# A graph layer in two convolutions: the first table holds max(x − mean, 0), and 1/std moves to a scale column

## The chip, the cores and the metric

One core of one Trainium2 chip. The metric is device time in microseconds (us) for one execution of the whole program. A core has five engines that run their own instruction streams beside each other: PE (TensorE, matmuls), DVE (VectorE), ACT (ScalarE), POOL (GpSimd, here the issuer of gathers) and SP (SyncE, here the issuer of all other DMAs).

## The reference

The input is x (6250 nodes × 512), and 100000 edges as src and dst, sorted by dst. With h = relu(layernorm(x)), deg the number of edges that leave a node, dinv = 1/sqrt(deg) and 0 where deg is 0, the program computes

```python
norm = -dinv[src] * dinv[dst]
prop = lambda h: segment_sum(h[src] * norm[:, None], dst)
a = h @ W1_0 + prop(h) @ W1_1 + b1
a = layer_norm(a) * gamma + beta
a = where(a >= 0, a, 0.01 * a)
out = x + a @ W2_0 + prop(a) @ W2_1 + b2
```

All of it is float32.

## The kernel before, in words

**Tiles.** The nodes are 49 blocks of 128 (the last has 106 rows), the edges 782 chunks of 128. Each of the two convolutions ("layers") has a table in DRAM with one row per node. Table 0 has rows of 512 + 16 floats: the row of h, and behind it a scale column, one float of which is used. Both layers run over the edges in order: POOL gathers the table rows of a chunk's 128 sources with one indirect DMA (L482), DVE makes a selection matrix for three chunks at a time that already holds the source's scale (L613 and on), PE sums the gathered rows into nodes by matmul (L668) and places the sums in blocks of nodes (L701); then each block is multiplied by the two weight matrices (L571), gets its bias and its layer norm (L754 to L785), and is stored into table 1.

**The prologue**, up to some 155 us, has to make the degrees, the layer norm of x, and table 0. x is loaded into places in SBUF in nine groups of blocks: 2, 4, 4, 4, 7, 7, 7, 7 and 6 (load_x, L185).

- *Degrees.* A loop of 25 iterations (L361 to L383, index g) counts src in two digits. Each makes two one-hot tiles on DVE (lo and hi, L365), and 16 matmuls on PE (both_ps, L382). Two buffers of one-hot tiles are in use, so DVE of iteration g + 2 waits for PE of iteration g. At g = 1 PE and ACT turn the src ids into per-partition indices for the gathers (turn_rest, L294: transposes L242, copies sidx L244), at g = 2 the dst ids (turn_dst, L298).
- *Statistics.* For the first 31 blocks ACT makes them (stats, L264): one pass for the sum (L269), one for the sum of squares (L273), then a square root for the group (L275). DVE turns this into 1/std and −mean/std (spread, L277: L280 and L281). For the last 18 blocks DVE makes them after the loop with bn_stats (L407 to L418).
- *Table.* make_table (L283) does relu(x · rs + nb) in place on ACT with a scale and a bias per node (L289), then SP stores two blocks at a time (L290), and then POOL may gather raw rows of x into the places just stored (gather_raw, L251). The first 76 chunks are gathered from x itself in this way, before the table is there; after the scales are known, the look-ups (L521 to L542) find the scale and bias of each of these rows and ACT applies relu to them.
- *Turns.* At certain iterations of the degree loop one group is finished: spread, make_table, one more load (load_rest), statistics of the group two further on. The dictionary at L339 gives them: iteration 1 the group 0, 4 the group 1, 7, 11, 17 and 21 the groups 2 to 5. The rest of the 31 blocks follows behind the loop.
- *Scales.* Behind the loop the counts are folded into deg; root = sqrt(max(deg, 1)) on ACT (L400), dinv, ndinv = −dinv and other columns on DVE. Then come the 18 other blocks, one DMA that writes dinv into the scale column of the first 31 blocks (L420, 3968 elements of 4 bytes), and the two products sc = (rs · dinv, nb · dinv) for the look-ups (L421 and L422). The column of the other 18 blocks is put into their places ahead of the store (L417).

**What sets the order.** On SP every DMA goes in the order in which the program issues it, and a waiting one holds those behind it. SP's order at the start is: x group 0, src ids, group 1, src ids by chunk, group 2, dst ids by chunk, groups 3, 4 and 5; after that what the turns issue. load_rest(k) loads group 6 + k for k below 3. It is called as load_rest(k − 1) in the turns k = 0 to 3, that is with −1, 0, 1 and 2. On ACT and DVE a scheduler interleaves the operations around the loop by priority; behind the prologue the orders of PE, POOL and SP are written out by hand.

**In layer 0** the scaled sum of a block is copied on ACT with the factor ndinv per node (an, L799), multiplied by W1_1 on top of h times W1_0, and DVE adds the bias (L768; for the last four blocks, which are begun early, L592).

Of the kernel before, what the change touches and what calls it, by code (L numbers as in the profile page):

```python
# [21 lines left out]
P = 128  # L22
# [22 lines left out]
def gnn_kernel(  # L45
# [71 lines left out]
    ndeg = const.tile([P, NB], F32, name="ndeg")  # L117
    ln = const.tile([P, 2, NB], F32, name="ln")
    dlx = const.tile([P, 1 + STEP * NQ * NS + 1], F32, name="dlx")
# [85 lines left out]
    load_end(chunks[1], dst)  # L205
    for i0, n in groups[3:6]:
        load_x(i0, n)

    def load_rest(k):
        if k < 3:  # L210
            load_x(*groups[6 + k])
        if k == 2:
            nc.sync.dma_start(tab[1][zero_row : zero_row + 1, :], places[P - 1 : P, RE + NB - 1, :D])
        for t, w in zip(w_sb[k - 3 : k - 2], (W1_1, W1_0)[k - 3 :]) if k >= 3 else ():
            nc.sync.dma_start(t, w.rearrange("(k p) d -> p k d", p=P))
        if k == 4:
            for t, v in ((bias1, b1), (bias2, b2), (gam, gamma), (bet, beta)):
                nc.sync.dma_start(t, dup(v, P))
# [39 lines left out]

    rs_all, nb_all = ln[:, 0, :], ln[:, 1, :]
    nm_all = ep.tile([P, NB], F32, name="nm_all")  # L260
    sq_all = ep.tile([P, NB], F32, name="sq_all")
    sums = ep.tile([P, NB], F32, name="sums")

    def stats(i0, n):  # L264

        cols = slice(i0, i0 + n)
        for i in range(i0, i0 + n):
            junk = ep.tile([P, D], BF, name="junk")
            nc.scalar.activation(junk, places[:, RE + i, :D], AF.Copy, accum_out=sums[:, i : i + 1])  # L269
        nc.scalar.activation(nm_all[:, cols], sums[:, cols], AF.Copy, scale=-1.0 / D)  # L270
        for i in range(i0, i0 + n):
            junk = ep.tile([P, D], BF, name="junk")
            nc.scalar.activation(junk, places[:, RE + i, :D], AF.Square, bias=nm_all[:, i : i + 1],  # L273
                                 accum_out=sq_all[:, i : i + 1])
        nc.scalar.activation(rs_all[:, cols], sq_all[:, cols], AF.Sqrt, bias=eps, scale=1.0 / D)  # L275

    def spread(i0, n):  # L277

        cols = slice(i0, i0 + n)
        nc.vector.reciprocal(rs_all[:, cols], rs_all[:, cols])  # L280
        nc.vector.tensor_mul(nb_all[:, cols], nm_all[:, cols], rs_all[:, cols])  # L281

    def make_table(i0, n):  # L283

        for lo in range(i0, i0 + n, 2):
            hi = min(lo + 2, i0 + n)
            for i in range(lo, hi):
                v = places[:, RE + i, :D]
                nc.scalar.activation(v, v, AF.Relu, bias=nb_all[:, i : i + 1], scale=rs_all[:, i : i + 1])  # L289
            nc.sync.dma_start(tab[0][lo * P : hi * P, :].rearrange("(i p) d -> p i d", p=P),  # L290
                              places[:, RE + lo : RE + hi, :])
            gather_raw(X + RE + lo, X + RE + hi)
# [45 lines left out]
    assert len(groups) == 9 and all(n > 0 for _, n in some + others)  # L338
    turns = {1: 0, 4: 1, 7: 2, 11: 3, 17: 4, 21: 5}  # L339
    with tc.issue_after(turned.ins):  # L340
        for k in range(2):
            stats(*some[k])

    both = ep.tile([P, NB, 2, 2], F32, name="both")
    with tc.tile_pool(name="deg", bufs=1) as dp, tc.tile_pool(name="onehot", bufs=2) as ohp, tc.tile_pool(
# [15 lines left out]
        for g in range(EJ // (2 * GJ)):  # L361
# [9 lines left out]
            if k is not None:  # L371
                spread(*some[k])
                make_table(*some[k])
                if k < 4:
                    load_rest(k - 1)
                if k + 2 < len(some):
                    stats(*some[k + 2])
            if g in (1, 2):
                with tc.tile_pool(name="turn_ps", bufs=3 - g, space=bass.MemoryType.PSUM) as wps:
                    (turn_rest, turn_dst)[g - 1](wps)  # L380
            for j in range(GJ):
# [3 lines left out]

    spread(*some[6])
    make_table(*some[6])

# [18 lines left out]
    for i0, n in others:  # L407
        cols = slice(i0, i0 + n)
        st = ep.tile([P, 7, 6], F32, name="st")
        mv = ep.tile([P, 7, 2], F32, name="mv")  # L410
        for j in range(n):
            nc.vector.bn_stats(st[:, j, :], places[:, RE + i0 + j, :D])
# [3 lines left out]
        nc.vector.scalar_tensor_tensor(nb_all[:, cols], mv[:, :n, 0], -1.0, rs_all[:, cols], op0=OP.mult, op1=OP.mult)  # L416
# [4 lines left out]
    nc.vector.tensor_mul(sc[:, 0, :], rs_all, dinv)  # L421
    nc.vector.tensor_mul(sc[:, 1, :], nb_all, dinv)  # L422

# [9 lines left out]
def usual_path(tc, have):  # L433
    nc = tc.nc
    (x, out, tab, root, ndeg, ndinv, sidx, dlx, iota_r, w_sb, W2_1, W2_0, w_late, ident, eps, ones, first, nodes_ps, node_of, minus,
     unsorted, dinv, sdinv, bias1, bias2, gam, bet, unseen, unit, N, E, D, NB, NC, NU, NS, KD, rows, places, R,
     load_rest, sc, pick, src_lo, src_hi, eidx, e_src, zero_row, p_id, lent, X, starts, src, W) = (
        have[n] for n in ("x out tab root ndeg ndinv sidx dlx iota_r w_sb W2_1 W2_0 w_late ident eps ones first nodes_ps node_of "
                          "minus unsorted dinv sdinv bias1 bias2 gam bet unseen unit N E D NB NC NU NS KD rows places "
# [13 lines left out]
    with ExitStack() as es:  # L453
# [131 lines left out]
        def early(layer, i):  # L585
# [5 lines left out]
            if layer == 0:  # L591
                nc.vector.tensor_add(pre[i][:r], u_ps[:r], bias1[:r])  # L592
# [161 lines left out]
        def finish(layer, i, v):  # L754
            r = rows[i]
            v = v[:r]
            if layer == 1:
# [8 lines left out]
                return  # L766
            if i < NB - 1:
                nc.vector.tensor_add(v, v, pre.pop(i)[:r] if i in EARLY else bias1[:r])  # L768
            st = pool.tile([P, 6], F32, name="st")
# [17 lines left out]
        def turn(layer, i, left=()):  # L787
# [7 lines left out]
            for k, aT in left:  # L795
# [565 lines left out]
```

## Time and profile before

| what | value |
|---|---|
| median of 3 runs | 2463.06 us (2460.94 to 2464.36) |
| the profiled execution: its own time | 2480.21 us |
| the profiled execution: its span | 2478.4 us |
| mean granted PE clock | 0.836 |

The profile comes from one further execution, with the profiler on. Its span runs from the first instruction to the last; 1.8 us of the execution's own time lie around it. Start times are counted from the start of the span. A row of the timeline gives start, duration, engine, line, operation, the tiles written and read, and in brackets how long the engine had been idle and what released it. A row of the groups gives busy us and mean ns, then the idle time ahead of them and its releasers. "places" are the blocks of x, the table rows and the gathered rows in turn; q1 is the queue of SP's DMAs, q0 that of the gathers.

### The profile page before, as it was taken

The page shows a single profiled execution, that of the slowest core. Times are in us where ns is not written, and L with a number is a line of the kernel's source. Part 1 is how long each engine was busy: PE and PEld are TensorE (multiplying, and loading weights), DVE is VectorE, ACT ScalarE, POOL GpSimd, SP SyncE. Part 2 cuts the span into 40 slices and gives each one's busy share as a digit, 9 for nine tenths or more (in the row PEclk, how much of TensorE's full clock was granted, in tenths as well). Part 3 has the DMA queues.
Part 4 walks back from the last instruction along what each step waited for, and adds up shares of the span by engine and source line. Part 5 has one row for each costly group of instructions (what it writes and reads, how often), then busy time and mean ns, then how long its engine had stood idle before and what let it go on. Part 6 is the DMA issues. An engine that isn't in the chain of part 4 may idle for free.

```text
span 2478.4 us, 19802 instructions
## 1 busy us (share of the span) xinstructions
PE 1719.3 (69%) x6907; PEld 710.0 (29%) x6907; DVE 678.2 (27%) x1449; ACT 390.7 (16%) x703; POOL 1494.4 (60%) x1578
## 2 busy tenths in 40 slices
PE   4567768576776766767766576766777767677788
PEld 3443223222222222223322122222232222222333
DVE  5954323132333322323333111111121111111121
ACT  5864111110111111111110000000010101000001
POOL 5455656666666666656645566666666666666560
PEclk7768878788888887889887688878889888888899
DMA  9885667667766776767645676766767677676670
GB/s 343 305 275 162 203 181 213 201 196 210 214 209 191 212 216 201 212 185 225 193 142 155 180 226 208 226 199 215 220 208 230 211 227 218 202 228 222 204 224 32
DMA packets 183086, 515.60 MB, mean 208 GB/s; under 512 B 33858, under 2 KB 35632, under 8 KB 182976
## 3 DMA queue, kind: packets, MB, share of 16 engines
q0 software_dynamic: 125120, 415.88, 56.5%
q1 hardware_dynamic: 57816, 98.34, 11.4%
q8 instruction: 56, 0.92, 0.1%
q14 instruction: 54, 0.44, 0.1%
q10 hardware_dynamic: 40, 0.02, 0.0%
HBM read 475.25 MB, written 38.86 MB: 207 GB/s over the span
## 4 chain that ended last, share of the span: by engine, by line
PE 33%; another core or an unknown queue 22%; issue 22%; POOL 9%; DVE 8%; DMA 4%; ACT 1%; DVEq 0%; SPq 0%; POOLq 0%; ACTq 0%
PE u_ps L571 16%; POOL places L482 9%; PE ps L668 8%; PE an_ps L701 5%; DMA places<-tab,sidx 2%; DMA places<-tab,lidx 2%; PE hT_ps L807 1%; PE hT_ps L559 1%; DVE aT L809 1%; DVE hi L365 1%; DVE there L689 1%; PE hT_ps L530 1%; DVE sel L613 1%; DVE lo L365 1%
## 5 line engine op out<-in xcount | busy, mean ns | idle before, releaser
L482 POOL DMA_INDIRECT places<-tab,sidx x1191 | 1136.5, 954 | 661.6 <-issue 304.8
L668 PE MATMUL ps<-places,sel 128*32 128x512 f32 x3104 | 426.1, 643 | 20.2 <-issue 19.6
L701 PE MATMUL an_ps<-agg,there 128*128 128x512 f32 (+1 forms) x554 | 277.0, 629 | 128.3 <-issue 91.7
L482 POOL DMA_INDIRECT places<-tab,lidx x270 | 256.0, 948 | 142.7 <-issue 67.9
L571 PE MATMUL u_ps<-w,aT 128*128 128x512 f32 x384 | 205.3, 684 | 154.2 <-DVE aT L809 91.0
L571 PE MATMUL u_ps<-places,aT 128*128 128x512 f32 x384 | 211.2, 700 | 130.0 <-DVE aT L809 110.6
L613 DVE TENSOR_TENSOR sel<-dlx,nodes_ps 128x384 f32<-128x384 f32 (+3 forms) x134 | 72.4, 542 | 699.0 <-remote 586.1
L571 PE MATMUL u_ps<-w,hT 128*128 128x512 f32 (+1 forms) x400 | 203.6, 655 | 34.4 <-ACT hT L561 30.1
L681 ACT ACTIVATE agg<-ps 128x512 f32<-128x512 f32 (+2 forms) x130 | 76.4, 590 | 950.0 <-remote 722.2
L571 PE MATMUL u_ps<-places,hT 128*128 128x512 f32 (+2 forms) x408 | 197.0, 629 | 16.8 <-ACT hT L561 16.2
L668 PEld LDWEIGHTS ps<-places,sel 128*32 128x32 f32 x3104 | 98.8, 116 | 326.8 <-issue 301.2
L701 PEld LDWEIGHTS an_ps<-agg,there 128*128 128x128 f32 (+1 forms) x554 | 104.7, 198 | 253.9 <-issue 221.5
L807 PE MATMUL hT_ps<-ident,an 128*128 128x128 f32 x384 | 69.6, 309 | 126.0 <-issue 65.1
L571 PEld LDWEIGHTS u_ps<-w,aT 128*128 128x128 f32 x384 | 81.0, 221 | 260.3 <-issue 154.8
L689 DVE TENSOR_SCALAR there<-iota_r,node_of 128x128 f32<-128x128 f32 (+1 forms) x286 | 82.3, 295 | 253.5 <-remote 115.6
L571 PEld LDWEIGHTS u_ps<-places,aT 128*128 128x128 f32 x384 | 82.5, 226 | 239.1 <-DVE aT L809 126.5
L561 ACT ACTIVATE hT<-hT_ps 128x512 f32<-128x512 f32 (+1 forms) x98 | 58.3, 595 | 449.7 <-remote 144.8
L571 PEld LDWEIGHTS u_ps<-w,hT 128*128 128x128 f32 (+1 forms) x400 | 80.6, 212 | 121.4 <-issue 90.0
L762 DVE SCALAR_TENSOR_TENSOR u_ps<-u_ps,root,bias 128x512 f32<-128x512 f32 x45 | 34.1, 759 | 289.1 <-issue 124.6
L571 PEld LDWEIGHTS u_ps<-places,hT 128*128 128x128 f32 (+1 forms) x408 | 80.4, 208 | 99.2 <-issue 81.1
L807 PEld LDWEIGHTS hT_ps<-ident,an 128*128 128x128 f32 x384 | 44.7, 152 | 209.8 <-issue 133.0
L253 POOL DMA_INDIRECT places<-in_x_dram,sidx x63 | 60.2, 955 | 68.3 <-issue 18.7
(196 smaller groups left out, 1217.9 us busy)
## 6 DMA issues: line engine op xcount, KB each, us to landing
h<-tab SPq DMA_DIRECT2D x90, 256.0 KB
places<-tab,sidx POOLq DMA_INDIRECT x1191
xt<-in_x_dram SPq DMA_DIRECT2D x48, 256.0 KB
out_dram<-t SPq DMA_DIRECT2D x48, 256.0 KB
tab<-t SPq DMA_DIRECT2D x46, 256.0 KB
tab<-places SPq DMA_DIRECT2D x22, 528.0 KB
places<-in_x_dram SPq DMA_DIRECT2D x5, 1792.0 KB
places<-tab,lidx POOLq DMA_INDIRECT x270
```

The lines of the kernel that those rows point to most:

```text
L253: nc.gpsimd.indirect_dma_start(out=lent[t] if t < X else places[:, t - X, :D], out_offset=None, in_=x, in_offset=bass.IndirectOffsetOnAxis ...
L365: nc.vector.tensor_tensor(t, s[:, g * 2 * GJ : (g + 1) * 2 * GJ].rearrange("p (j s) -> p j s", s=2)[:, :, None, :] .to_broadcast([EP, GJ, ...
L482: nc.gpsimd.indirect_dma_start(out=places[:, slot(t), :] if own_scale else zr(layer, t), out_offset=None, in_=x if layer == 0 and t < RAW ...
L561: nc.scalar.activation(hT[:, :, :r], ps[:, :, :r], AF.Copy)
L571: nc.tensor.matmul(u_ps[:r], hT[:, kc, :r], w[:, kc, :], start=(start and kc == 0), stop=(stop and kc == KD - 1))
L613: nc.vector.tensor_tensor(sel[:, q : q + k, :w, :], of, node[:, q : q + k, None, :].to_broadcast([P, k, w, Q]), op=OP.is_equal)
L668: nc.tensor.matmul(to, sel[:, q, s, :], rows_of, start=(s == 0), stop=(s == len(chunk[q]) - 1 and (cnt is None or chunk[q][0] >= AHEAD_OF)))
L681: nc.scalar.activation(agg[g][: n * Q, lo : lo + w], ps[: n * Q, lo : lo + w], AF.Copy)
L689: behind[1] = nc.vector.tensor_scalar(t[:m, :r], iota_r[:m, :r], node_of[:m, g : g + 1], -(1.0 + i * P), op0=OP.subtract, op1=OP.is_equal)
L701: nc.tensor.matmul(placed[i][:r], t[:m, :r], agg[g][:m, :], start=(g == inside[i][0]), stop=(g == inside[i][-1]))
L762: nc.vector.scalar_tensor_tensor(v, v, root[:r, i : i + 1], bias2[:r], op0=OP.mult, op1=OP.add)
L807: nc.tensor.transpose(ps[:, kc, :r], an[:r, kc * P : (kc + 1) * P], ident[:r, :r])
```

## The change

- Table 0's rows become max(x − mean, 0): relu with a bias (−mean) alone. Since 1/std is positive, h = max(x − mean, 0)/std.
- 1/std goes elsewhere: into the scale column as dinv/std; into the look-ups' sc (rs · dinv, −mean · rs · dinv), as before in value; and into the bias addition of layer 0, which becomes u · (1/std) + bias. As that multiplies the propagated part too, the copy of the placed sum has the factor ndst = ndinv · std in place of ndinv. The last four blocks keep ndinv.
- spread is gone. One square root on ACT over 31 columns (std) stands behind the loop, and one reciprocal behind the other blocks. A group's relus need its sums only.
- Groups 0 to 3 of x are loaded ahead; group 4 + k is loaded behind the stores of turn k, for k = 0 to 4. There are seven turns, at iterations 1, 3, 6, 9, 13, 18 and 22, and the statistics run one group ahead. The dst ids are turned at g = 5.
- The scale column of the first 31 blocks is written with 16 equal floats (64 bytes) per node, from a tile that DVE fills.

```diff
-        nc.scalar.activation(rs_all[:, cols], sq_all[:, cols], AF.Sqrt, bias=eps, scale=1.0 / D)
-
-    def spread(i0, n):
-
-        cols = slice(i0, i0 + n)
-        nc.vector.reciprocal(rs_all[:, cols], rs_all[:, cols])
-        nc.vector.tensor_mul(nb_all[:, cols], nm_all[:, cols], rs_all[:, cols])
...
-                nc.scalar.activation(v, v, AF.Relu, bias=nb_all[:, i : i + 1], scale=rs_all[:, i : i + 1])
+                nc.scalar.activation(v, v, AF.Relu, bias=nm_all[:, i : i + 1])
...
-    for i0, n in groups[3:6]:
-        load_x(i0, n)
+    load_x(*groups[3])
 
     def load_rest(k):
-        if k < 3:
-            load_x(*groups[6 + k])
...
-    turns = {1: 0, 4: 1, 7: 2, 11: 3, 17: 4, 21: 5}
+    turns = {1: 0, 3: 1, 6: 2, 9: 3, 13: 4, 18: 5, 22: 6}
...
-                spread(*some[k])
                 make_table(*some[k])
-                if k < 4:
-                    load_rest(k - 1)
-                if k + 2 < len(some):
-                    stats(*some[k + 2])
-            if g in (1, 2):
+                if 4 + k < len(groups):
+                    load_x(*groups[4 + k])
+                if k == 5:
+                    load_rest(2)
+                if k + 1 < len(some):
+                    stats(*some[k + 1])
+            if g in (1, 5):
...
-    spread(*some[6])
-    make_table(*some[6])
+    early = NB - LAST
+    nc.scalar.activation(std[:, :early], sq_all[:, :early], AF.Sqrt, bias=eps, scale=1.0 / D)
...
-        nc.scalar.activation(rs_all[:, cols], mv[:, :n, 1], AF.Sqrt, bias=eps)
-        nc.vector.reciprocal(rs_all[:, cols], rs_all[:, cols])
-        nc.vector.scalar_tensor_tensor(nb_all[:, cols], mv[:, :n, 0], -1.0, rs_all[:, cols], op0=OP.mult, op1=OP.mult)
-        nc.vector.tensor_copy(places[:, RE + i0 : RE + i0 + n, D : D + 1], dinv[:, cols, None])
+        nc.scalar.activation(std[:, cols], mv[:, :n, 1], AF.Sqrt, bias=eps)
+        nc.vector.tensor_scalar_mul(nm_all[:, cols], mv[:, :n, 0], -1.0)
+        nc.vector.reciprocal(rs_all[:, cols], std[:, cols])
+        nc.vector.tensor_tensor(places[:, RE + i0 : RE + i0 + n, D : D + 1], dinv[:, cols, None], rs_all[:, cols, None],
+                                op=OP.mult)
         make_table(i0, n)
-    early = NB - LAST
-    nc.sync.dma_start(tab[0][: early * P, D : D + 1].rearrange("(i p) o -> p i o", p=P), dinv[:, :early, None])
+    nc.vector.reciprocal(rs_all[:, :early], std[:, :early])
     nc.vector.tensor_mul(sc[:, 0, :], rs_all, dinv)
-    nc.vector.tensor_mul(sc[:, 1, :], nb_all, dinv)
+    nc.vector.tensor_mul(sc[:, 1, :], nm_all, sc[:, 0, :])
+    nc.vector.tensor_mul(ndst, ndinv, std)
+    column = edges.enter_context(tc.tile_pool(name="column", bufs=1)).tile([P, early, PAD], F32, name="column")
+    nc.vector.tensor_copy(column, sc[:, 0, :early, None].to_broadcast([P, early, PAD]))
+    nc.sync.dma_start(tab[0][: early * P, D:].rearrange("(i p) o -> p i o", p=P), column)
...
-            if i < NB - 1:
-                nc.vector.tensor_add(v, v, pre.pop(i)[:r] if i in EARLY else bias1[:r])
+            if i not in EARLY:
+                nc.vector.scalar_tensor_tensor(v, v, ln[:r, i : i + 1], bias1[:r], op0=OP.mult, op1=OP.add)
+            elif i < NB - 1:
+                nc.vector.tensor_add(v, v, pre.pop(i)[:r])
...
-                                 scale=(ndeg if layer == 1 and i not in EARLY else ndinv)[:r, i : i + 1])
+                                 scale=(ndinv if i in EARLY else ndeg if layer else ndst)[:r, i : i + 1])
```

More of the change, by code (lines that the diff above doesn't have):

```diff
@@ L338, in gnn_kernel @@
     assert len(groups) == 9 and all(n > 0 for _, n in some + others)
-    turns = {1: 0, 4: 1, 7: 2, 11: 3, 17: 4, 21: 5}
+    turns = {1: 0, 3: 1, 6: 2, 9: 3, 13: 4, 18: 5, 22: 6}
     with tc.issue_after(turned.ins):
-        for k in range(2):
-            stats(*some[k])
+        stats(*some[0])
     both = ep.tile([P, NB, 2, 2], F32, name="both")
@@ L434, in usual_path @@
     nc = tc.nc
-    (x, out, tab, root, ndeg, ndinv, sidx, dlx, iota_r, w_sb, W2_1, W2_0, w_late, ident, eps, ones, first, nodes_ps, node_of, minus,
+    (x, out, tab, root, ndeg, ndst, ln, ndinv, sidx, dlx, iota_r, w_sb, W2_1, W2_0, w_late, ident, eps, ones, first, nodes_ps, node_of, minus,
      unsorted, dinv, sdinv, bias1, bias2, gam, bet, unseen, unit, N, E, D, NB, NC, NU, NS, KD, rows, places, R,
      load_rest, sc, pick, src_lo, src_hi, eidx, e_src, zero_row, p_id, lent, X, starts, src, W) = (
-        have[n] for n in ("x out tab root ndeg ndinv sidx dlx iota_r w_sb W2_1 W2_0 w_late ident eps ones first nodes_ps node_of "
+        have[n] for n in ("x out tab root ndeg ndst ln ndinv sidx dlx iota_r w_sb W2_1 W2_0 w_late ident eps ones first nodes_ps node_of "
                           "minus unsorted dinv sdinv bias1 bias2 gam bet unseen unit N E D NB NC NU NS KD rows places "
@@ L591, in early @@
             if layer == 0:
-                nc.vector.tensor_add(pre[i][:r], u_ps[:r], bias1[:r])
+                nc.vector.scalar_tensor_tensor(pre[i][:r], u_ps[:r], ln[:r, i : i + 1], bias1[:r], op0=OP.mult, op1=OP.add)
             else:
```

10 lines of the change are left out of this document (6 added, 4 removed).

## The prediction

> **What bounds the kernel now.** I read the page's totals and its chain first, then a table by stage, then the timeline of the stages that stood out.
>
> ```profile
> span 2478.4 us, 19802 instructions
> PE 1719.3 (69%) x6907; PEld 710.0 (29%) x6907; DVE 678.2 (27%) x1449; ACT 390.7 (16%) x703; POOL 1494.4 (60%) x1578
> PE 33%; another core or an unknown queue 22%; issue 22%; POOL 9%; DVE 8%; DMA 4%; ACT 1%; DVEq 0%; SPq 0%; POOLq 0%; ACTq 0%
> ```
>
> PE leads and DVE and ACT are mostly idle: over the whole span, the operations that the change saves on DVE and ACT would be worth nothing. The stages say where they could count. Columns: stretch, length, busy us of each engine with its instructions, granted PE clock, DMA share, GB/s.
>
> ```profile
> core 0: us, PE busy (x) PEld busy (x) DVE busy (x) ACT busy (x) POOL busy (x), PEclk, DMA share, GB/s
> 18.00:41.10 23.10, 3.72 (x18) 2.54 (x18) 3.81 (x11) 2.35 (x9) 14.77 (x16) 0.56 1.04 397
> ...
> 75.00:93.00 18.00, 12.52 (x102) 10.79 (x101) 17.93 (x16) 17.36 (x45) 3.79 (x4) 0.78 0.67 220
> 93.00:107.30 14.30, 8.65 (x80) 7.68 (x78) 14.16 (x14) 9.70 (x16) 7.09 (x8) 0.90 0.81 262
> 107.30:125.60 18.30, 3.23 (x32) 2.57 (x31) 14.71 (x57) 11.31 (x19) 11.73 (x13) 0.56 1.01 376
> ...
> 132.00:141.40 9.40, 6.16 (x18) 2.63 (x17) 0.05 (x1) 2.93 (x4) 6.49 (x7) 0.68 1.05 377
> 141.40:155.00 13.60, 7.26 (x36) 6.52 (x36) 8.40 (x17) 9.27 (x14) 3.79 (x4) 0.50 0.68 145
> ...
> 157.00:1300.00 1143.00, 805.95 (x3176) 323.90 (x3168) 359.48 (x822) 183.61 (x313) 701.28 (x734) 0.84 0.68 200
> ```
>
> From 157 us on, layer 0 runs with DVE at 31% (359.48 of 1143), and layer 1 after it is not touched. The first 155 us, the prologue, are serial with it: nothing of the main loop can start before the scales are known. So a change of the prologue's end passes to the end of the kernel about one to one. In it there are four stages: almost nothing runs from 18 to 41 us but the DMAs; DVE is full from 41 to 107; to 125.6 it makes degrees and statistics; from 132 to 141 everything but the DMAs stands again.
>
> ```profile
> 9.08 1.21 DVE L365 TENSOR_TENSOR lo<-s_lo,iota_w 125x2048 bf16<-125x2048 bf16 x1
> ...
> 26.24 1.68 PE L382 MATMUL both_ps<-hi,lo 125*128 125x196 bf16 x9
> ...
> 41.06 1.22 DVE L365 TENSOR_TENSOR lo<-s_lo,iota_w 125x2048 bf16<-125x2048 bf16 x1 [19.30 <-remote]
> ...
> 52.31 1.22 DVE L365 TENSOR_TENSOR lo<-s_lo,iota_w 125x2048 bf16<-125x2048 bf16 x1
> ...
> 55.14 1.22 DVE L365 TENSOR_TENSOR lo<-s_lo,iota_w 125x2048 bf16<-125x2048 bf16 x1
> ...
> 105.49 1.78 DVE L365 TENSOR_TENSOR hi<-s_hi,iota_w 125x3136 bf16<-125x3136 bf16 x1
> ...
> 112.36 0.25 ACT L400 ACTIVATE root<-root 128x49 f32<-128x49 f32 x1 [2.09 <-DVE st L412]
> ...
> 125.49 0.21 DVE L422 TENSOR_TENSOR sc<-ln,dinv 128x49 f32<-128x49 f32 x1
> ...
> 141.43 0.57 DVE L536 TENSOR_TENSOR an<-u_ps,t 128x392 f32<-128x392 f32 x1 [9.38 <-remote]
> ...
> 158.89 1.01 POOL L482 DMA_INDIRECT places<-tab,sidx  x1 [0.60 <-issue]
> ...
> 182.94 0.66 PE L559 MATMUL hT_ps<-ident,h 128*128 128x128 f32 x4 [3.07 <-issue]
> ```
>
> The wait of 19.30 us ends with no instruction that the trace names; PE's nine matmuls had been done by its records at about 28 us. Both standstills (19.3 and 9.4 us) lie where the DMA share is 1.04 and 1.05. They are the largest things in the prologue, and what ends them isn't shown.
>
> **The change, part by part.** (1) *Spreads gone.* Seven reciprocals and seven multiplications leave DVE, seven square roots leave ACT.
>
> ```profile
> L280 DVE RECIPROCAL ln<-ln 128x4 f32<-128x4 f32 (+3 forms) x7 | 1.2, 176 | 0.0
> L281 DVE TENSOR_TENSOR ln<-nm_all,ln 128x4 f32<-128x4 f32 (+3 forms) x7 | 1.1, 160 | 0.0
> L289 ACT ACTIVATE places<-places,ln 128x512 f32<-128x512 f32 x49 | 35.8, 802 | 11.2 <-DVE ln L281 6.9 <-issue 1.4 <-DVE ln L416 1.2
> L318 DVE COPY first<-nodes_ps 128x265 f32<-128x265 f32 x1 | 0.4, 436 | 1.6 <-PE nodes_ps L317 1.6
> L421 DVE TENSOR_TENSOR sc<-ln,dinv 128x49 f32<-128x49 f32 x1 | 0.2, 203 | 0.0
> ```
>
> On full DVE that is 1.2 + 1.1 = 2.3 us. A pure iteration of the one-hot loop takes 55.14 − 52.31 = 2.83 us; 22 of them are 62.3 us, and 41.06 to 107.27 is 66.2. Five spreads (5 × 0.336 = 1.7) and the 2.2 us of small operations of turning dst make up the rest; the latter stay, only at g=5 in place of g=2. ACT also loses the 6.9 us for which its relus waited for a spread.
>
> (2) *Scale work behind the loop.* Added on DVE ahead of the look-ups: a reciprocal of 31 columns (0.2), ndst (0.2, as L421), and the column's copy of 128x496, by L318 0.436 × 496/265 = 0.8: 1.2 us. The negated means take the place of one three-operand operation per group, the scaled column that of a copy: nothing. So sc comes 2.3 − 1.2 = 1.1 us earlier from DVE's side.
>
> (3) *x behind stores.* SP keeps 14 blocks up front in place of 28; groups 4 to 8 each go behind the stores of a turn.
>
> ```profile
> 10.44 9.61 SPq L189 DMA_DIRECT2D places<-in_x_dram  x3
> 20.16 9.73 SPq L290 DMA_DIRECT2D tab<-places  x1
> 43.33 0.37 SPq L189 DMA_DIRECT2D places<-in_x_dram  x1
> ```
>
> ```profile
> SPq L189 <- DMA places<-in_x_dram: 13.4, 1, 13.4
> ```
>
> ```profile
> DMA packets 25826, 48.88 MB, mean 315 GB/s; under 512 B 5910, under 2 KB 7472, under 8 KB 25816
> ...
> q0 software_dynamic: 6000, 19.67, 35.8%
> ```
>
> Here the diff removes more than it says. In the turn k=0 the kernel before calls load_rest(k − 1) = load_rest(−1), which is load_x(groups[5]): seven blocks are loaded a second time at 43.33, after SP waited 13.4 us for the first load of the same places. 7 × 128 × 2048 bytes = 1.8 MB go, the wider column adds 3968 × 60 = 0.24 MB: −1.6 MB of 48.88. At the 397 GB/s of the saturated stage that is 3.9 us of transfer. It counts, because from 107 to 141 the DMAs are saturated and the second standstill ends with that: −3.9 us if nothing else moves. More can come: from 75 to 107 the DMAs run at 220 and 262 GB/s because the stores wait for ACT, whose relus now follow the statistics of their block at once. The upper end is the whole second standstill and the 1.1 us, 10.5.
>
> ```profile
> L269 ACT ACTIVATE junk<-places 128x512 bf16<-128x512 f32 x31 | 19.4, 627 | 2.4 <-DMA places<-in_x_dram 1.8
> ...
> L273 ACT ACTIVATE junk<-places,nm_all 128x512 bf16<-128x512 f32 x31 | 22.4, 721 | 0.8
> ```
>
> What ACT loses against this: it has statistics of one group ahead in place of two, so about 4 blocks less are done when the first standstill ends. A block costs 0.627 + 0.721 + 0.802 = 2.15 us, with the reading of its sums some 2.3 (an estimate). At 41 us 25 whole blocks, 4 relus and about 5 us of small operations are left: 57.5 + 3.2 + 5, to 107. The root's square root (L400) stands behind all of it in ACT's order; it ran at 112.36 and would now be wanted at about 110. ACT has 3 us of room, so the early stores may gain but the scales gain little. I take −6.5, between 3.9 and 10.5, nearer to the lower end.
>
> (4) *The column of 64 bytes*, bounds from packets of other sizes:
>
> ```profile
> q1 hardware_dynamic: 4061, 0.23, 41.8%
> ```
>
> ```profile
> q1 hardware_dynamic: 828, 0.44, 50.5%
> ```
>
> ```profile
> q1 hardware_dynamic: 3000, 5.99, 67.5%
> ```
>
> The first is 139 to 148 us, the 4-byte column: 0.418 × 9 us × 16 / 4061 = 14.8 ns a packet. The second is 16 to 19 us, where 512-byte ids are loaded: 0.505 × 3 × 16 / 828 = 29 ns. The third is 50 to 75 us, 2 KB rows: 90 ns. 64 bytes lie next to the first: I take 15 ns, so nothing. 29 ns would double 9 us to 18 and the landing at 148 to 157, still ahead of the first gather of a table row at 158.89; 90 ns is a rival.
>
> The Trainium skill bears on this, "DMA: Bandwidth & Descriptors", section "Specifications": transfers below 512 bytes are done by reading, changing and writing back. By that 64 bytes escape it no more than 4 did, which speaks against a gain from wider packets, and the sum by it is the same; no packet of 64 bytes to DRAM stands by itself in this trace.
>
> (5) *Layer 0's blocks.* The bias addition becomes scale and add.
>
> ```profile
> L762 DVE SCALAR_TENSOR_TENSOR u_ps<-u_ps,root,bias 128x512 f32<-128x512 f32 x45 | 34.1, 759 | 289.1 <-issue 124.6
> ```
>
> ```profile
> L768 DVE TENSOR_TENSOR u_ps<-u_ps,bias 128x512 f32<-128x512 f32 x43 | 30.1, 699 | 205.4 <-issue 82.0 <-PE u_ps L571 74.4 <-PE ps L668 25.4
> ```
>
> 0.06 us × 45 = 2.7 us on DVE, 31% busy there. The finish is not on PE's order, so PE covers it: 0; without cover +2.7. The relu on ACT keeps its time (one pass of 128x512, a constant scale), ndst in place of ndinv is the same read.
>
> Sum: −6.5 us on the profiled execution, 2480.2 → 2473.7. That execution took 17.1 us more than the median of 2463.06; I carry the difference over: **2456.5 us**, own range 2452 to 2460.
>
> **The rivals.** *The first standstill goes* (fewer bytes are queued at its start, so it ends sooner). For it: it lies just where the long loads sit in the queue (three loads take 9.61 us to issue, the next store 9.73). Against it: the raw gathers fill the DMAs as well, and saturation alone does not stop DVE. Then DVE's loop ends at 9.1 + 25 × 2.83 + 2.2 = 82, sc at about 101, and the DMAs decide: 47.3 MB at 397 GB/s are 119 us, with 4 us for dips 123, and the 13.6 us of the stage from 141.4 to 155 behind it: 137 in place of 155, −18: 2445.
>
> *ACT becomes late* (the slower side). x of groups 4 to 8 is now behind stores that wait for ACT itself, so ACT may wait for x that waited for ACT. Place: the sums over a group (L269), before which ACT waited only for its first blocks. A load of 1.8 MB at half of 397 GB/s takes 9.3 us. If three of the five are exposed in full, ACT ends 28 − 3 = 25 us later than it may; less the 6.5 of the forecast, +18.5: 2481.5. It decides from a wait of 3 + 6.5 = 9.5 us in all. Against it: each load is issued a whole group's work (7 × 2.3 = 16 us) or more before its use.
>
> *The column's packets cost like rows*: 248 per engine, each 90 ns beside a gather's packet on q0 (0.358 × 155 × 16 / 6000 = 148 ns), 59 us; issued at about 122 it lands at 181, and the rows of h behind it at about 183. PE wants them first at 182.94, in the forecast 6.5 us earlier: −6.5 + 6.5, 2463.
>
> *The change doesn't do what it says*: both standstills come from outside the program, in the profiled execution only, and the prologue of the timed runs has another end: 0 to −4, 2461.
>
> **How the numbers follow.** A measurement of this kernel tells 0.2%, 4.9 us, from no change: faster is below 2458.1, slower above 2468.0. Forecast 0.40, of which 0.28 lies below 2458.1; standstill gone 0.28; ACT late 0.15; column 0.07; nothing 0.10. Faster 0.28 + 0.28 = 0.56, slower 0.15 (ACT late), same 0.12 + 0.07 + 0.10 = 0.29. The range 2443 to 2468 takes in the forecast, the column, nothing, and most of the first rival; it leaves out 0.05 of that one and 0.14 of ACT's: 0.19.
>
> **What would show it.** Right: SP's wait of 13.4 us and the second load of seven blocks gone; one iteration 2.83 us throughout; no wait of ACT for DVE in the relus; the root's square root at 106 to 111 us; DMAs in the 75 to 107 stretch above 300 GB/s; the second standstill shorter and over by 135; sums from about 148. Wrong: the wait for "remote" at 41 us gone or halved (first rival); ACT L269's groups waiting for DMAs of x by more than 9 us (second); the column's packets above 40 ns (third); and, beyond all rivals, a stage behind 157 us that takes longer, DVE's scale and add on PE's path above all.

## The result and the profile after

The changed kernel is slower: a median of 2482.8 us (20 runs) against 2465.15 us (20 runs of the kernel before); the ratio is 1.0071, 95% interval 1.0046 to 1.0096, so +11 to +24 us. This ratio and those below leave out executions that took over 1.5% longer than the fastest of the same kernel (one of b_burst's below, 4149 us, among them). The forecast was 2456.5 us, −0.27%, with a range that ended at 2468. The profiled execution took 2492.07 us, 11.9 more than that of before.

The totals and the chain of the changed kernel's page:

```profile
span 2490.3 us, 19786 instructions
PE 1712.1 (69%) x6907; PEld 704.5 (28%) x6907; DVE 682.2 (27%) x1438; ACT 380.0 (15%) x697; POOL 1492.2 (60%) x1578
...
PE 34%; issue 24%; another core or an unknown queue 15%; POOL 13%; DMA 5%; DVE 5%; ACT 3%; SPq 0%; POOLq 0%; DVEq 0%; ACTq 0%
```

ACT is busy for 10.7 us less, and DVE for 4 us more. As before, nothing of that tells where 12 us come from. The stages give a first hint (same stretches as before):

```profile
core 0: us, PE busy (x) PEld busy (x) DVE busy (x) ACT busy (x) POOL busy (x), PEclk, DMA share, GB/s
...
18.00:41.10 23.10, 3.22 (x14) 1.96 (x14) 1.86 (x2) 2.93 (x9) 17.15 (x19) 0.52 1.02 382
...
75.00:93.00 18.00, 11.77 (x96) 10.22 (x95) 15.29 (x11) 17.72 (x44) 8.53 (x9) 0.81 1.03 364
93.00:107.30 14.30, 7.92 (x64) 6.96 (x64) 11.49 (x8) 9.78 (x24) 6.63 (x7) 0.76 0.92 314
107.30:125.60 18.30, 9.50 (x64) 7.78 (x64) 14.52 (x29) 2.41 (x6) 2.84 (x3) 0.61 0.26 86
...
141.40:155.00 13.60, 0.00 (x0) 0.00 (x0) 0.76 (x2) 0.00 (x0) 10.20 (x11) 0.50 1.08 342
...
157.00:1300.00 1143.00, 844.94 (x3269) 338.28 (x3268) 376.04 (x852) 196.52 (x336) 699.62 (x734) 0.86 0.68 201
```

Two stretches are new. From 75 to 107 us DVE, which was full, has holes, while the DMAs move 364 and 314 GB/s in place of 220 and 262. And from 141 us on PE, DVE and ACT do nothing until 154.2. The timeline names the second (the rows come from the timelines of single engines and of all engines; "remote" means that the trace names no instruction that ended the wait):

```profile
44.39 1.22 DVE L356 TENSOR_TENSOR lo<-s_lo,iota_w 125x2048 bf16<-125x2048 bf16 x1 [24.53 <-remote]
...
93.88 1.22 DVE L356 TENSOR_TENSOR lo<-s_lo,iota_w 125x2048 bf16<-125x2048 bf16 x1 [3.56 <-remote]
...
108.69 1.22 DVE L356 TENSOR_TENSOR lo<-s_lo,iota_w 125x2048 bf16<-125x2048 bf16 x1 [3.28 <-remote]
...
116.98 1.78 DVE L356 TENSOR_TENSOR hi<-s_hi,iota_w 125x3136 bf16<-125x3136 bf16 x1
122.89 0.25 ACT L392 ACTIVATE root<-root 128x49 f32<-128x49 f32 x1 [19.95 <-DVE root L391]
134.94 0.21 DVE L414 TENSOR_TENSOR sc<-nm_all,sc 128x49 f32<-128x49 f32 x1
135.07 0.66 DVE L417 COPY column<-sc 128x496 f32<-128x496 f32 x1
141.61 1.14 SPq L418 DMA_DIRECT2D tab<-column  x1
154.24 1.41 DVE L514 TENSOR_SCALAR xt<-ps,p_id 128x512 f32<-128x512 f32 x2 [18.51 <-DMA tab<-column]
155.04 2.03 PE L526 MATMUL u_ps<-sc,xt 128*128 128x98 f32 x8 [31.39 <-DMA tab<-column]
...
168.04 0.62 PE L664 MATMUL ps<-w,sel 128*32 128x512 f32 x2
```

The same two rows of the kernel before, first look-up and sums:

```profile
125.62 1.40 DVE L518 TENSOR_SCALAR xt<-ps,p_id 128x512 f32<-128x512 f32 x2
...
155.03 1.07 PE L668 MATMUL ps<-w,sel 128*32 128x512 f32 x2
```

L514 makes the first selection matrix of the look-ups. It reads nothing of the column. In the kernel before, its row started at 125.62 us, 0.1 us behind sc; here it waits 18.5 us for the column's DMA. The tile of the column is in a pool that is closed, with the other tiles of the prologue, just ahead of the look-ups, and the look-ups' pool takes over that space. I infer that its first tile, xt, lies where the column lay (the profile shows no addresses; the experiments below test it). Then it may not be written until the DMA has read the column; and that DMA stands on SP behind ten table stores (issued at 141.61, 5.9 us after the copy was done) and then moves its 3968 packets among the gathers. First sums come at 168.0 in place of 155.0.

### The profile page after: what moved, and what is told of

The parts are those of the page before. It is cut to its first block, busy times and chain, and to the rows that moved or that the text cites. A ratio compares the mean times of both kernels' runs of the same rounds, so it can differ in the third digit from the quotient of the medians.

```text
span 2490.3 us, 19786 instructions
## 1 busy us (share of the span) xinstructions
PE 1712.1 (69%) x6907; PEld 704.5 (28%) x6907; DVE 682.2 (27%) x1438; ACT 380.0 (15%) x697; POOL 1492.2 (60%) x1578
## 3 DMA queue, kind: packets, MB, share of 16 engines
q1 hardware_dynamic: 56904, 96.74, 11.2%
## 4 chain that ended last, share of the span: by engine, by line
PE 34%; issue 24%; another core or an unknown queue 15%; POOL 13%; DMA 5%; DVE 5%; ACT 3%; SPq 0%; POOLq 0%; DVEq 0%; ACTq 0%
PE u_ps L567 15%; POOL places L478 13%; PE ps L664 9%; PE an_ps L697 6%; DMA places<-tab,sidx 4%; PE hT_ps L805 1%; PE hT_ps L555 1%; DVE hi L356 1%; DMA places<-tab,lidx 1%; PE both_ps L374 1%; DMA tab<-column 1%; ACT places L281 0%; DVE aT L807 0%; DVE lo L356 0%
## 5 line engine op out<-in xcount | busy, mean ns | idle before, releaser
L664 PE MATMUL ps<-places,sel 128*32 128x512 f32 x3104 | 443.1, 655 | 30.6 <-issue 30.0
L697 PE MATMUL an_ps<-agg,there 128*128 128x512 f32 (+1 forms) x554 | 284.1, 642 | 177.4 <-issue 131.4
L567 PE MATMUL u_ps<-places,aT 128*128 128x512 f32 x384 | 195.5, 656 | 84.0 <-DVE aT L807 81.8
L567 PE MATMUL u_ps<-w,aT 128*128 128x512 f32 x384 | 193.4, 651 | 73.0 <-DVE aT L807 65.0
L567 PE MATMUL u_ps<-places,hT 128*128 128x512 f32 (+2 forms) x408 | 202.7, 645 | 43.8 <-ACT hT L557 43.2
L805 PE MATMUL hT_ps<-ident,an 128*128 128x128 f32 x384 | 71.5, 315 | 159.8 <-issue 135.1
L567 PEld LDWEIGHTS u_ps<-places,aT 128*128 128x128 f32 x384 | 77.1, 211 | 181.6 <-DVE aT L807 92.6
L764 DVE SCALAR_TENSOR_TENSOR u_ps<-u_ps,ln,bias 128x512 f32<-128x512 f32 x45 | 34.1, 759 | 280.7 <-issue 107.4
```

Source lines behind the costliest of these rows:

```text
L567: nc.tensor.matmul(u_ps[:r], hT[:, kc, :r], w[:, kc, :], start=(start and kc == 0), stop=(stop and kc == KD - 1))
L664: nc.tensor.matmul(to, sel[:, q, s, :], rows_of, start=(s == 0), stop=(s == len(chunk[q]) - 1 and (cnt is None or chunk[q][0] >= AHEAD_OF)))
L697: nc.tensor.matmul(placed[i][:r], t[:m, :r], agg[g][:m, :], start=(g == inside[i][0]), stop=(g == inside[i][-1]))
L764: nc.vector.scalar_tensor_tensor(v, v, ln[:r, i : i + 1], bias1[:r], op0=OP.mult, op1=OP.add)
L805: nc.tensor.transpose(ps[:, kc, :r], an[:r, kc * P : (kc + 1) * P], ident[:r, :r])
```

## The experiments

Times stand as ratios to runs of the kernel before on the same chip. The chips differ: those with a granted clock of 0.84 (2430 to 2500 us; all runs above too; two chips in this table) and a single one of 0.92 (2014 to 2040 us). At 0.84 a ratio is known to about 0.3%, at 0.92 to 0.1%.

| run | kernel | chip | ratio (95%) | sc, first xt, sums (us) |
|---|---|---|---|---|
| before | before | 0.84 | 1 | 125.4, 125.6, 155.0 |
| after | the change | 0.84 | 1.0071 (1.0046 to 1.0096) | 134.7, 154.2, 168.0 |
| a_pad | change, column in places | 0.84 | 1.0022 (0.9997 to 1.0046) | 134.9, 138.9, 163.5 |
| a_pad2 | the same again | 0.84 | 1.0020 (0.9983 to 1.0058) | 135.1, 139.1, 165.1 |
| a_narrow | change, 4 bytes, no tile | 0.84 | 1.0008 (0.9984 to 1.0031) | 134.1, 138.1, 162.1 |
| b_wide | before + tile of the column | 0.84 | 1.0038 (1.0013 to 1.0063) | 135.9, 157.1, 172.4 |
| b_wide2 | the same again | 0.84 | 1.0011 (0.9982 to 1.0040) | 137.3, 158.7, 172.9 |
| b_turns | before + loads and turns | 0.84 | 0.9999 (0.9968 to 1.0029) | 134.5, 134.8, 159.9 |
| b_once | before, no second load | 0.84 | 1.0024 (0.9983 to 1.0065) | 133.3, 133.6, 158.5 |
| b_gate | before, 14 gathers held | 0.84 | 1.0003 (0.9962 to 1.0044) | 111.2, 111.5, 143.7 |
| b_burst | before, 14 gathers at g = 9 | 0.84 | 1.0018 (0.9984 to 1.0052) | 137.6, 137.9, 162.1 |
| a_narrow_early | change's arithmetic alone | 0.84 | 1.0036 (1.0002 to 1.0070) | 138.5, 142.5, 165.6 |
| a_best | a_narrow, nm_all moved | 0.84 | 1.0014 (0.9981 to 1.0047) | 133.5, 133.6, 150.9 |
| before2 | before | 0.92 | 1.0003 (0.9992 to 1.0013) | 105.7, 106.0, 120.2 |
| after2 | the change | 0.92 | 1.0074 (1.0054 to 1.0094) | 99.8, 124.9, 139.2 |
| a_narrow2 | change, 4 bytes, no tile | 0.92 | 0.9975 (0.9964 to 0.9986) | 99.3, 103.3, 117.4 |
| a_narrow_gate | a_narrow + 14 held | 0.92 | 0.9972 (0.9963 to 0.9981) | 99.6, 103.7, 118.7 |
| a_narrow_gate2 | the same again | 0.92 | 0.9976 (0.9966 to 0.9985) | 99.6, 103.5, 118.0 |
| a_narrow_early_gate | a_narrow_early + 14 held | 0.92 | 0.9985 (0.9976 to 0.9994) | 101.8, 105.8, 121.0 |
| b_gate_once | b_gate, no second load | 0.92 | 0.9995 (0.9984 to 1.0006) | 105.0, 105.2, 119.2 |

"sc" is the start of the first of its two products, "sums" the second group of sums on PE. Each row of starts is one profile. At 0.84 such profiles differ without any change: b_wide and b_wide2 are the kernel before up to sc, but for the column's DMA, and have it at 135.9 and 137.3 in place of 125.4. So there a few us between two profiles show nothing. The wait of the changed kernel for its column was one theory (A); the other (B) was that the loss is made in the degree loop, which ends at 118.7 us in place of 107.3.

**The column without its tile.** a_pad fills the free floats behind the places and stores from there, a_narrow stores sc itself:

```diff
-    column = edges.enter_context(tc.tile_pool(name="column", bufs=1)).tile([P, early, PAD], F32, name="column")
-    nc.vector.tensor_copy(column, sc[:, 0, :early, None].to_broadcast([P, early, PAD]))
-    nc.sync.dma_start(tab[0][: early * P, D:].rearrange("(i p) o -> p i o", p=P), column)
+    nc.vector.tensor_copy(places[:, RE : RE + early, D:], sc[:, 0, :early, None].to_broadcast([P, early, PAD]))
+    nc.sync.dma_start(tab[0][: early * P, D:].rearrange("(i p) o -> p i o", p=P), places[:, RE : RE + early, D:])
```

```diff
+    nc.sync.dma_start(tab[0][: early * P, D : D + 1].rearrange("(i p) o -> p i o", p=P), sc[:, 0, :early, None])
```

> The changed kernel, but the 64-byte column is filled in the free floats behind the places of the first 31 blocks and stored from there, so no tile of its own lies in space that the look-ups' first tile (xt, L514) takes over. Theory A (the look-ups wait for the column's DMA, 18.5 us, because xt lies in the column's space): this wait is gone, xt follows sc at once, the sums start 10 to 18 us earlier than 168, time 2465 to 2473. Theory B (the loss is made in the degree loop, whose end moved from 107 to 118.7 us, and the DMAs are full until 157 anyway): 0 to -4, 2479 to 2483.

> The changed kernel with a column of 4 bytes, stored straight from sc, without a tile. Theory A (waiting for the column's tile): like the kernel with the column in the free floats, within 3 us, 2465 to 2473. Rival (64-byte packets are dear in themselves): another 5 us or more below that one. Theory B: 2479 to 2483.

> The changed kernel with the 64-byte column filled in the places and stored from there. Theory A with packets of equal price: no wait for the column's DMA, ratio as with the 4-byte column, 0.997 to 0.999 on a chip of 0.90 or more, 1.000 to 1.002 on one of 0.84. Rival (64-byte packets dear): 0.2% or more above that.

In all three the wait for the column is gone and the loss falls to 0.08 to 0.22%, which can't be told from none. The two widths don't differ by more than the intervals. In these profiles the sums start only 2.9 to 5.9 us earlier than in the changed kernel, not the 10 to 18 expected; in a_pad, for one, a wait of 7.3 us for "remote" follows, to 157.8 us. The row of a_narrow shows what is left ahead of the first look-up:

```profile
138.05 1.41 DVE L512 TENSOR_SCALAR xt<-ps,p_id 128x512 f32<-128x512 f32 x2 [3.53 <-ACT places L281]
```

**The tile alone, in the kernel before.** The three lines of the column, as in the diff of the change, with dinv in place of sc.

> The kernel before, with nothing changed but the column: 64 bytes per node of dinv, from a tile in a pool of its own that is closed before the look-ups, stored behind the table. Theory A: the first xt waits for this DMA, to some 148 us in place of 127; 9.4 us of that replace the second standstill, so +8 to +13, 2473 to 2478. Theory B: no change, within 3 us of 2465.

> The kernel before with the 64-byte column from a closed pool's tile, on the chip of the next two. Theory A: the first xt waits 17 to 24 us for the column's DMA, and the whole change of sign is in it. On a chip of 0.90 or more: ratio 1.007 to 1.011. On one of 0.84, where part of it replaces a standstill: 1.003 to 1.007. Rival: within 0.1%.

```profile
157.08 1.41 DVE L520 TENSOR_SCALAR xt<-ps,p_id 128x512 f32<-128x512 f32 x2 [20.84 <-DMA tab<-column]
```

The wait is there (20.8 and 21.1 us; the row is b_wide's) and the sums start at 172 to 173 us. b_wide's ratio, 1.0038, is some 9 us, as expected (8 to 13); b_wide2's, 1.0011, is lower than expected and doesn't lie clear of 1, though its medians, 2471.87 against 2461.80 us, lie 10 us apart. So theory A's mechanism is shown by adding and by taking away; its price at 0.84 is less sure than at 0.92, below.

**Loads and turns alone, the second load alone, the arithmetic alone.** b_turns takes the diff of load_x, load_rest and turns, and keeps spreads and column. b_once has `if 0 < k < 4` ahead of load_rest(k − 1). a_narrow_early is a_narrow with loads and turns of before, without the second load.

> The kernel before with the loads and turns of the changed one (14 blocks of x ahead, groups 4 to 8 behind stores, seven turns, dst ids at g = 5, no second load), spreads and narrow column kept. Theory B: the loop ends about 11 us later, sc at about 135 instead of 125.5, +8 to +12, 2473 to 2477. Theory A: the later loop is made up by the missing second standstill (the DMAs drain at the same time): within 4 us of 2465.

> The kernel before without the second load of seven blocks of x, nothing else. By the prediction's third part: 1.8 MB less, -3.9 us, 2461 to 2463. Rival (loads of x are not what the prologue's end waits for): within 2 us of 2466.

> The changed kernel's arithmetic alone: rows max(x - mean, 0), 1/std in the scale column and in layer 0's bias addition; loads, turns and dst ids at the places of the kernel before, without its second load; column of 4 bytes straight from sc. Against the kernel before without the second load: 14 small DVE operations less, 1 us of scale work more, 2.7 us of DVE in layer 0: by the prediction -1 to -4, 2458 to 2464. Rival (the added operations stand on the path behind the loop, or layer 0's scale and add is not covered): +2 to +5, 2464 to 2470.

b_turns: 0.9999; theory B's 8 to 12 us aren't there, though its loop ends at 115.0 us. b_once: nothing that this chip can tell. a_narrow_early: +0.36%, some 9 us and above both expectations, but only just clear of 1, with a wait of DVE of 15.4 us in the loop, to 109.3 us, that the kernel before hadn't. It lies in a run of 17 gathers on POOL, from 86.7 to 108.1 us.

**What the standstills hang on.** The timelines of POOL gave a third theory (G): the first standstill ends some 4 to 5 us behind the last of 26 gathers that POOL issues one upon the other (before: last one at 36.40, DVE goes on at 41.06).

```profile
36.40 0.95 POOL L253 DMA_INDIRECT places<-in_x_dram,sidx  x1 [0.30 <-issue]
```

b_gate holds 14 of them, one per iteration; b_burst has its copy and its gathers at `if g == 9`, for all 14 together. The diff of b_gate:

```diff
-    gather_raw(0, X + RE)
+    gather_raw(0, X)
...
+            if 3 <= g < 3 + RE:
+                nc.vector.tensor_copy(places[:EP, g - 3, :1], hot[-1][:, 0, :1])
+                gather_raw(X + g - 3, X + g - 2)
```

> The kernel before with the first run of raw gathers cut from 26 to 12: the other 14 go one per iteration of the degree loop from g = 3 on, each held by a copy of one column from that iteration's one-hot tile into its place. Theory G (PE's releases come late as long as POOL issues one gather after another, and the standstill ends some 4 to 5 us behind the run's last gather): the run ends at about 23.5 us in place of 37, DVE goes on at about 28 in place of 41, the loop ends near 95. As the DMAs still have their bytes to move, -5 to -14, 2452 to 2461. Rival S (the standstill belongs to the start, or to the bytes of x in the queue): DVE goes on at about 41, 2463 to 2469. Rival R (it is made by the recording of the profile): the profile shows it gone, the time stays, 2463 to 2469.

> Like the one with gathers held, but all 14 are released together at g = 9. Theory G: the first standstill is over by about 28 us, and a second one of 10 to 17 us appears in the loop while POOL issues the 14 and those behind them; loop end within 5 of 107, time 2461 to 2467. Rival S' (only the start is disturbed): no standstill in the loop, as with gathers one by one, 2452 to 2461.

b_gate, DVE's longest waits for a one-hot buffer in the loop:

```profile
18.87 1.22 DVE L365 TENSOR_TENSOR lo<-s_lo,iota_w 125x2048 bf16<-125x2048 bf16 x1 [3.67 <-remote]
...
58.65 1.22 DVE L365 TENSOR_TENSOR lo<-s_lo,iota_w 125x2048 bf16<-125x2048 bf16 x1 [1.74 <-remote]
69.48 1.22 DVE L365 TENSOR_TENSOR lo<-s_lo,iota_w 125x2048 bf16<-125x2048 bf16 x1 [2.08 <-remote]
...
83.37 1.22 DVE L365 TENSOR_TENSOR lo<-s_lo,iota_w 125x2048 bf16<-125x2048 bf16 x1 [2.16 <-PE both_ps L385]
```

b_burst, DVE, and then the last gather of its run on POOL (26 from 48.16 on):

```profile
84.72 1.22 DVE L365 TENSOR_TENSOR lo<-s_lo,iota_w 125x2048 bf16<-125x2048 bf16 x1 [26.61 <-remote]
```

```profile
79.42 0.95 POOL L253 DMA_INDIRECT places<-in_x_dram,sidx  x1 [0.30 <-issue]
```

The standstill goes with the run and comes back with it, ending 5.3 us behind its last gather; with 26.6 us it is longer than the 10 to 17 expected, and b_burst's loop ends at 118.4, not near 107. In the profile of b_gate the loop ends at 95.0 and the sums start at 143.7, 11 us sooner; the time, 1.0003 with 0.4% to both sides, can't confirm these 11 us. The medians of all runs on this chip, 2451.15 for b_gate and 2457.86 for the kernel before, lie 6.7 us apart, so whether holding the gathers gains time stays open. In the changed kernel the loop's later end, 11.5 us, is made up of 3.3 us by which the first standstill ends later and of three holes of 3.6, 3.3 and 1.4 us at 94, 109 and 113. The holes lie by runs of 7 and 10 gathers. One may argue that relus which wait for no spread release stores and thereby gathers sooner, and so make longer runs. This isn't shown: no run takes these holes away alone, the kernel before has a run of 9 from 98 us on without a hole in its loop, and b_turns has runs of 7 with a hole of 1.3 us at most.

**The same kernels on the chip of 0.92.** The first three expectations were worked out from profiles at 0.84.

> The changed kernel with the 4-byte column straight from sc, and 14 of the first 26 raw gathers held, one per iteration of the degree loop from g = 3 on. Theory G (standstills come with long runs of gathers): the first standstill shrinks from 24 us to below 8; the loop, which ends at 119 us without the hold, ends before 105; sums before 152 in place of 162; time 8 to 14 us below the kernel with the 4-byte column alone, ratio to before 0.996 to 0.999. Against it: the turns' gathers and the held ones may join into a new long run, then the loop ends at 110 to 119 and the ratio is 1.000 to 1.002.

> The changed kernel's arithmetic with loads and turns of before (without the second load), 4-byte column, and the 14 gathers held. Without the hold it had two standstills in the loop (22.9 us at 20, 16.6 us at 94) and its loop ended at 123.7. Theory G: the first shrinks below 8, the second stays or shrinks as its run is not longer; loop end 100 to 110, sums 147 to 155, ratio 0.996 to 1.000. Rival (the early relus alone delay the loop): loop end above 115, ratio as without the hold, 1.003.

> The kernel before with the 14 gathers held, and without the second load of x. With the hold alone its profile had the loop's end at 95 and the sums at 143.7. Theory: the same loop end, the DMAs drain up to 4.5 us earlier, sums at 139 to 144; 11 to 16 us less than before, ratio 0.993 to 0.996. Rival R (the first standstill is made by the recording alone): ratio 0.998 to 1.002 though the profile shows sums at 144 or sooner.

> The kernel before, unchanged, for its profile on the chip of the next three. Theory G as seen so far: DVE stands from 21 to 41 us, until 4 to 5 us behind the last of 26 gathers; loop end 107, sums 155. Rival C (the standstill belongs to some chips): if this chip grants 0.90 or more, no wait above 8 us, loop end 83 to 88, sums near 120; time 1.000.

> The changed kernel, unchanged, on the same chip. Theory A: first xt 17 to 20 us behind sc, waiting for the column's DMA, on any chip. On a chip of 0.84: loop end 119, ratio 1.005 to 1.009. On one of 0.90 or more (rival C): loop end near 85 and the wait for the column alone, sums 8 to 18 us later than in the kernel before, ratio 1.004 to 1.009.

> The changed kernel with the 4-byte column straight from sc, on the same chip. Theory A: no wait for the column. On a chip of 0.84 what is left is the later loop, ratio 1.000 to 1.003. On one of 0.90 or more there is no standstill to pay for, and the forecast's own terms are left (less bytes, no spreads): ratio 0.996 to 0.999.

> The same with the 14 gathers held. On a chip of 0.84, theory G: first standstill below 8 us, ratio 0.994 to 0.998. On one of 0.90 or more: nothing to gain from the hold against the kernel without it, within 0.1% of it, 0.997.

before2, the stretch of the first standstill, and its first look-up and sums:

```profile
18.00:41.10 23.10, 13.52 (x115) 10.99 (x115) 17.70 (x27) 18.09 (x50) 14.27 (x16) 0.85 1.04 394
```

```profile
105.99 1.40 DVE L518 TENSOR_SCALAR xt<-ps,p_id 128x512 f32<-128x512 f32 x2
...
120.23 0.62 PE L668 MATMUL ps<-w,sel 128*32 128x512 f32 x2
```

after2 and a_narrow2:

```profile
100.05 0.21 DVE L414 TENSOR_TENSOR sc<-nm_all,sc 128x49 f32<-128x49 f32 x1
124.89 1.41 DVE L514 TENSOR_SCALAR xt<-ps,p_id 128x512 f32<-128x512 f32 x2 [24.06 <-DMA tab<-column]
...
139.24 0.62 PE L664 MATMUL ps<-w,sel 128*32 128x512 f32 x2
```

```profile
99.53 0.21 DVE L414 TENSOR_TENSOR sc<-nm_all,sc 128x49 f32<-128x49 f32 x1
103.33 1.41 DVE L512 TENSOR_SCALAR xt<-ps,p_id 128x512 f32<-128x512 f32 x2 [3.59 <-ACT places L281]
...
117.41 0.62 PE L662 MATMUL ps<-w,sel 128*32 128x512 f32 x2
```

Here DVE is busy for 17.7 of the 23.1 us with the same run of gathers (16 in the stretch) at 394 GB/s: no standstill, and holding the gathers gains nothing (0.9972 and 0.9976 with, 0.9975 without). So neither the run nor full DMAs suffice; what differs in the chips isn't shown. The granted clock of the stretch, 0.85 here and 0.56 before, doesn't settle it: from 107 to 125 us in after2, where PE waits for the column, it is 0.50 on this chip too, so a low value may follow from a standstill. b_gate_once, expected at 0.993 to 0.996, came out at 0.9995: on this chip neither the hold nor the second load's bytes are worth what was forecast. The changed kernel has its sc 5.8 us earlier than before2 (100.05 against 105.87 for its second product), waits 24.1 us, and loses 0.74%; without the wait it gains 0.25%. Between them lie 0.99% of 2021.7 us, 20 us, and 21.8 us in the start of the sums.

**A second wait of the same kind.** In a_narrow the first xt waits 3.5 us for ACT's last relus. They read nm_all, whose space is also given up with the prologue. a_best puts nm_all into the pool that stays open.

> The changed kernel with the 4-byte column straight from sc, and nm_all in the pool that stays open in place of the one that is closed before the look-ups. If the 3.5 us for which the first xt waits for ACT's last relus (they read nm_all) is the same kind of wait, it goes, sums start 2 to 4 us earlier, ratio 0.1% to 0.2% below the kernel with the 4-byte column: 0.995 to 0.997 on a chip of 0.90 or more, 0.998 to 1.001 on one of 0.84. Rival (the look-ups' results wait for ACT anyway, as it works on relus until then): no gain, 0.9975.

```profile
133.61 0.74 DVE L512 TENSOR_SCALAR xt<-ps,p_id 128x512 f32<-128x512 f32 x1
```

xt then follows sc at once (133.6 behind 133.5), and the sums start at 150.9 in place of 162.1, more than the 3.5 us of the wait can account for. The time, on a chip of 0.84, is 1.0014 with 0.3% to both sides: inconclusive. Versions that beat both kernels are there on the chip of 0.92 only: a_narrow, 0.9975, with the hold or without.

## Why the prediction was wrong

- **The step that failed is (2) with (4).** The column was priced as a copy on DVE (0.8 us; it took 0.66) and as packets of a DMA, and the only one to wait for it was the gather of a table row. That its tile takes space that the next stage writes first wasn't looked for: the wait for it was put at nothing. The rule was in the prediction's own reach: where a change adds a tile, ask who gets its space and what has then to be done with it. The price is the wait, 18.5 us in the profile on a chip of 0.84 and 24.1 on one of 0.92; in time about 0.56% (1.0071 less the mean of a_narrow and a_pad, 14 us) and 0.99% (20 us). With it gone the change is no longer slower beyond the intervals at 0.84; why it isn't faster there stays open.
- **The forecast's own −6.5 us** is matched where the wait is taken away on the chip of 0.92: a_narrow2, 0.9975, −5.0 us (−2.8 to −7.3). That is luck, since it is made up differently. Its larger part was (3), less bytes and so a shorter second standstill; before2 has no second standstill to shorten, and b_gate_once, without the second load (and with the hold), gains between −1.2 and 3.2 us where (3) counted 3.9 for the bytes. The prediction also let the turning of the dst ids cost the same at g = 5 as at g = 2. In before2 DVE waits 4.4 us at g = 2 for these ids to be loaded:

```profile
23.52 0.63 DVE L310 TENSOR_SCALAR dst_c<-dst_c 128x896 f32<-128x896 int32 x1 [4.43 <-DMA dst_c<-in_dst_dram]
```

  In a_narrow2 the same operation, at 27.1 us, waits for nothing, and the loop ends at 84.4 us in place of 89.5; 3.6 us are lost again in xt's wait for ACT, and the sums start 2.8 us earlier. This is read from one profile of each; no run moves the dst ids alone. On a chip of 0.84 no gain is to be seen: a_narrow 1.0008 ± 0.0023. Two sizes differ as well: the relu without a scale per node took 0.708 us, not 0.802, where the prediction let it keep its time; and ACT, for which it saw 3 us of room, was done with the first 31 blocks at 102.9 us, while DVE's loop stood for 34.0 us in all:

```profile
L281 ACT ACTIVATE places<-places,nm_all 128x512 f32<-128x512 f32 x49 | 32.6, 708 | 0.3 <-DVE nm_all L407 0.3
...
L356 DVE TENSOR_TENSOR lo<-s_lo,iota_w 125x2048 bf16<-125x2048 bf16 x25 | 30.4, 1217 | 34.0 <-remote 32.8 <-PE fT L240 1.0
```

- **Rival "ACT late"**, the slower side, is refuted: the sums over a group (L268) waited 0.5 us for x, and root's square root waited 19.95 us for DVE. The side was right by luck, the place wrong.
- **Rival "first standstill goes"** is refuted: 24.5 us in place of 19.3, and in b_turns, with 14 blocks of x ahead in place of 28, it is 21.8: the bytes of x in the queue don't set it.
- **Rival "column's packets cost like rows"** is refuted. In after2, 118 to 125 us, they are nearly all of q1:

```profile
q1 hardware_dynamic: 2633, 0.18, 26.3%
```

  0.263 × 7 × 16 / 2633 = 11.2 ns, far from 90. The prediction's 14.8 ns for 4 bytes has some 90 larger packets in it; by the trace's own records of the column's packets, those of 64 bytes took 11 ns in the median and on average (after2), those of 4 bytes 9 ns in the median and 12.9 on average (before). The rule of the Trainium skill on transfers below 512 bytes ("DMA: Bandwidth & Descriptors", section "Specifications") can't be told from this.
- **Rival "standstills from outside"** may be half of the truth. In the profiles of 0.84 the first standstill is there whenever the first run of gathers isn't cut, in those of the one chip of 0.92 never; whether it is as long without the recording stays open, since b_gate's 11 us didn't show in its time.
- **(5)** held: L764 takes 0.759 us on 128x512, as forecast, and at 0.92 the profiled kernels take 1897.4 us (after2), 1897.0 (a_narrow2) and 1897.0 (before2) from the start of the sums to the end. At 0.84 this stretch can't tell: 2322.3 (after) and 2323.4 (before), but 2294 to 2323 over all profiles.
- **(1) and (3)** did what they say to the program (second load and SP's wait of 13.4 us gone, no wait for spreads; from 75 to 107 us the DMAs move over 300 GB/s, as the prediction wanted to see), but that they bring time isn't shown: b_turns and b_once can't be told from 1.

## What to carry to other kernels

A tile that a DMA reads late, in a pool that is closed ahead of the next stage, makes the next stage's first tile wait for that DMA and for all that stands before it in its queue: look at who takes over the space, and store from a tile that stays. Price a new DMA not only by its packets but by everyone who waits for its source. And where a time hangs on waits whose releaser the trace doesn't name, compare on more than one chip, and in more than one profile, before an explanation is believed.

## What the runs showed of the hardware

On chips with a granted clock of 0.84, DVE waited up to 26.6 us for a release that the trace doesn't name (by the program's order, of a buffer that PE reads) while POOL issued a long run of gathers; on one chip of 0.92 the same program had no such wait, and the whole kernel took 2022 us in place of 2465. A 64-byte packet to DRAM took 11 ns, one of 4 bytes 9 ns in the median.
